# Nine inputs of a chain of attentions turned by VectorE and transfers instead of TensorE

## The chip, the cores and the metric

The kernel runs on one core of a Trainium2 chip. The metric is the time of one execution on the device, in microseconds. All arithmetic is in float32; the scores of two of the three layers use products in which a float32 is split in a high and a low part.

## The reference

Sixteen batches of 256 tokens with 256 features pass three attentions and a feed-forward layer. Softmax, norms and heads are the usual ones; the mask is all ones.

```python
def _L0_xattn_ref(query, context, context_mask, Wq, Wk, Wv, Wo, g_q, g_c, g_out):
    ...
    Q = (q_norm @ Wq)   # 16 heads of 16 features
    K = (c_norm @ Wk)
    V = (c_norm @ Wv)
    ...
    attn = jax.nn.softmax(scores, axis=-1)
    ...
    return rmsnorm(query + out, g_out)

def _forward(x, y, ...):
    h = _ln(x, ln1_g, ln1_b)
    q, k, v = ...                      # of h; q and k are rotated (rope)
    a = _attn(q, k, v, causal=True)
    x = x + (a @ sa_wo + sa_bo)
    h = _ln(x, ln2_g, ln2_b)
    q = ...                            # of h; k and v of y
    a = _attn(q, k, v, causal=False)
    x = x + (a @ ca_wo + ca_bo)
    h = _ln(x, ln3_g, ln3_b)
    return x + (jax.nn.gelu(h @ fc1_w + fc1_b) @ fc2_w + fc2_b)
```

Layer 0 is the cross attention with rms norms, layer 1 the causal self attention, layer 2 the cross attention to y. The last stage is the feed-forward layer, 256 to 1024 to 256.

## The kernel before

There are 48 attentions, 0 to 47: 3 layers by 16 batches. ORDER says which layer each number belongs to, so that the batches run as staggered pipelines: attention 5 is layer 1 of batch 0, 38 is layer 1 of batch 13, 47 is layer 2 of batch 15, the last. The feed-forward layer follows for pairs of batches (class Mlp, 8 pairs); its products are arranged as seven products instead of eight per level (up 1 to 7, down 1 to 7), with sums formed by VectorE (mix, sum_a).

Nothing is left to a scheduler. Each attention is cut in named words: stats, norm, q, k, v, four steps of scores (three for the causal layer), values, take_last, sums_in, heads_in, invert, divide, project, finish. A word is a generator with a step for each engine's part. The string PLAN lists 2640 such steps by name; the kernel walks through it and each word named does its next step. So PLAN is the order of every engine's queue at once: TensorE runs the first steps of q, k, v, scores, values and project in the order in which they stand there, and an instruction whose input is late holds up all that is behind it on its engine. SP's DMA queue is in order in the same way. Behind PLAN stands the code of the last stage, a loop over the pairs.

A layer's input x lies with tokens in the partitions. The products by q, k and v need it with features in the partitions, so after norm (L555) the tile xn must be turned. There are two ways:

- turn: four TensorE transposes with the identity into one PSUM bank (turn_ps, L570), and one copy to the tile hT (turn_out, L577), by ScalarE for attentions and by VectorE for the pairs 0 and 1.
- pieces: VectorE transposes blocks of 32 by 32 (pieces, L586, two instructions for an input), one transfer writes the tile bits to the DRAM tensor turn_hop (pieces_out, L594), and four transfers read it back so that the blocks come to the right partitions (pieces_in, L600). All five transfers are on SP's queue.

Before the change 15 inputs are turned (attentions 5, 12, 18, 22, 31, 38, 43, 45, 47, and both inputs of the pairs 0, 1 and 2) and 33 go in pieces (23 attentions and five pairs). The third pair is turned in the loop of the last stage, later pairs go in pieces there.

The scores (L955, L966) fill a PSUM tile for each half of the heads in a step; the pool psS has two such tiles, so one step fills it. ScalarE empties each with an exponential (L978), then values (L1009) multiplies the result with V. Other transfers on SP's queue bring the parts of q and k to the pairs of rows that the split products read (q_out L842, k_out L889), the heads and sums of an attention to the layout of the projection (heads_in L1032, sums_in L1043), and the inverses of the sums through DRAM (invert L1056, L1062; inv_hop, inv). divide (L1069) multiplies, project (L647) is the product with the output weights.

Of the kernel before, what the change touches and what calls it, by code (L numbers as in the profile page):

```python
# [55 lines left out]
scores.0.1 stats_x.2 values.0.0 q.1 scores.0.2 stats_y.2 v.1 scores.0.2 stats_y.2 scores.0.2  # L56
stats_x.3 values.0.1 load_piece.5.0 scores.0.3 stats_x.2 k.1 scores.0.3 stats_x.3 send.2 stats_y.3
scores.0.3 k.2 v.1 load_piece.5.1 v.1 send.2 k.1 values.0.1 send.3
scores.1.0 k_high.2 k_low.2 load_early.4 q.2 scores.1.0 send.3 scores.1.0 values.0.2 receive.2
load_early.3 scores.1.1 k_out.2 values.0.3 scores.1.1 q.3 q.2 scores.1.1 take_last.0 load_early.0  # L60
q_high.2 scores.1.2 q_low.2 values.1.0 scores.1.2 q_low.2 heads_in.0 v.2 v.2 stats_y.6 scores.1.2
q_out.2 scores.1.3 v.2 sums_in.0 k.3 stats_x.6 scores.1.3 receive.3 scores.1.3 load.4 values.1.1
k_high.3 values.1.1
scores.2.0 invert.0 values.1.2 k_low.3 scores.2.0 q.3 values.1.3 scores.2.0 heads_in.0 take_last.1
q_high.3 scores.2.1 invert.0 v.3 v.3 k_out.3 q_low.3 stats_x.6 scores.2.1 q_low.3 sums_in.1
scores.2.1 stats_y.3 values.2.0 stats_x.4 scores.2.2 stats_x.4 q_out.3 k.4 scores.2.2
load_piece.6.0 send.4 v.3 send.4 scores.2.2 load_piece.5.3 values.2.1 send.6 divide.0 k_high.4
stats_y.4 scores.2.3 invert.0 q.4 invert.1 scores.2.3 k_low.4 scores.2.3 receive.4 invert.1
stats_x.8 values.2.1
scores.3.0 heads_in.1 stats_x.8 values.2.2 scores.3.0 heads_in.1 fold_of_att load_piece.6.1  # L70
scores.3.0 q.4 load_early.2 load_later.1 values.2.3 divide.0 stats_y.4 q_high.4 invert.1
scores.3.1 send.8 take_last.2 project.0 scores.3.1 q_low.4 k_out.4 q_low.4 scores.3.1 values.3.0
project.0 fold_of_att q_out.4 scores.3.2 project.0 v.4 v.4 divide.1 scores.3.2 stats_y.8 project.0
scores.3.2 values.3.1 load_piece.5.2 finish.0 fold_of_att load_piece.7.2 scores.3.3 stats.5
values.3.1 k.6 scores.3.3 v.4 stats.5 scores.3.3 values.3.2 load_piece.7.0 sums_in.2 norm.5
k_high.6
scores.4.0 load_piece.7.1 k_low.6 values.3.3 scores.4.0 divide.1 fold_of_att turn.5 take_last.3
scores.4.0 send.6 project.1 fold_of_att turn.5 sums_in.3 invert.2 scores.4.1 heads_in.2 divide.2
project.1 load_later.0 q.5 project.1 scores.4.1 heads_in.2 fold_of_att project.1 scores.4.1
values.4.0 invert.2 invert.3 q.5 load_piece.6.2 scores.4.2 finish.1 heads_in.3 k.5 scores.4.2 q.5  # L80
q.5 load_early.1 scores.4.2 invert.3 values.4.1 q.5 receive.6 k.5 q.5 scores.4.3 k_out.6
values.4.1 q.6 k.5 q.5 q.5 invert.2 k.5 scores.4.3 v.5 v.5 stats_y.6 k.5 scores.4.3 k.5 heads_in.3
load_piece.6.3 values.4.2 q.6 stats.7
scores.5.0 q_high.6 values.4.3 stats.7 q_low.6 scores.5.0 v.6 q_low.6 scores.5.0 take_last.4
scores.5.0 q_out.6 divide.2 scores.5.0 send.8 scores.5.1 v.5 divide.3 v.6 norm.7 project.2
# [265 lines left out]
def xattn_kernel(  # L351
# [744 lines left out]
    def run(steps):  # L1096
        for _ in steps or ():
            pass
# [57 lines left out]
    class Mlp:  # L1156
# [31 lines left out]
        def pieces_out(self):  # L1188
            self.hops = [pieces_out(pieces(xn)) for xn in self.xns]
# [328 lines left out]
    with tc.manual_schedule():  # L1518
# [38 lines left out]
        for g in range(B // 2):  # L1557
# [56 lines left out]
            if third is not None:  # L1614
                third.pieces_out()
# [451 lines left out]
```

## Time and profile before

| | |
|---|---|
| median of 3 runs | 880.16 us (880.13 to 881.4) |
| the profiled execution | 880.08 us, its span 878.4 us |
| TensorE busy | 867.9 us, 99% of the span |
| VectorE busy | 660.0 us, 75% |
| ScalarE busy | 593.4 us, 68% |
| GpSimd busy | 352.9 us, 40% |
| granted TensorE clock | 1.00 |
| attention stage (PLAN) | to about 672 us |
| last stage | about 672 us to the end |

A row of the profile names the line, the engine, the operation and the tiles; x is the number of instructions, then come busy time, mean duration in ns, and the idle time of the engine just before them with what ended it. A float32 product shows as two records, a transpose by TensorE as one. In a timeline, the first number is the start in the span and the second the duration. SPq is the DMA queue of SyncE: its durations are those of issuing, not of the transfer.

### The profile page before, as it was taken

How to read it: one execution, taken by the hardware profiler on the slowest of the kernel's cores; microseconds unless marked ns; L12 is line 12 of the kernel's file. 1: busy time of each engine (PE TensorE's matmuls, PEld its weight loads, DVE VectorE, ACT ScalarE, POOL GpSimd, SP SyncE). 2: the span in 40 equal slices, each digit the busy share in tenths (PEclk: the TensorE clock that was granted, in tenths of full speed). 3: DMA queues.
4: the chain of work that ended last, by engine and by line, in shares of the span. 5: the costliest groups of instructions: out<-in, count | busy, mean ns of one | idle time of the engine just before them, and what ended most of it. 6: DMA issues, size and time to landing. Idle time of an engine off the chain costs nothing.

```text
span 878.4 us, 32887 instructions
## 1 busy us (share of the span) xinstructions
PE 867.9 (99%) x13762; PEld 558.9 (64%) x13762; DVE 660.0 (75%) x1487; ACT 593.4 (68%) x848; POOL 352.9 (40%) x558
## 2 busy tenths in 40 slices
PE   8999999999999999999999999999999999999997
PEld 4455555555555555555555555555556899999997
DVE  5368888888787878788776788888784787787562
ACT  4788767877787877788777787788876733333440
POOL 4154685257355357264555534334152132222000
PEclk9999999999999999999999999999999999999999
DMA  8576465455344345443343333224331022211201
GB/s 275 182 225 189 134 182 178 148 164 167 117 153 131 110 138 169 144 132 118 126 134 125 113 115 131 95 83 155 124 110 52 14 72 73 67 55 30 69 25 51
DMA packets 101454, 107.04 MB, mean 122 GB/s; under 512 B 26602, under 2 KB 81778, under 8 KB 101298
## 3 DMA queue, kind: packets, MB, share of 16 engines
q1 hardware_dynamic: 96210, 89.89, 31.1%
q0 software_dynamic: 4400, 14.42, 5.6%
q8 instruction: 110, 1.80, 0.9%
q10 hardware_dynamic: 688, 0.54, 0.2%
q14 instruction: 46, 0.38, 0.1%
HBM read 46.33 MB, written 13.65 MB: 68 GB/s over the span
## 4 chain that ended last, share of the span: by engine, by line
PE 86%; DVE 4%; DMA 3%; issue 2%; SPq 2%; ACT 2%; POOL 1%; ACTq 0%; DVEq 0%; POOLq 0%
PE d L647 17%; PE d L635 16%; PE A L1009 15%; PE S L966 8%; PE upX L1223 6%; PE S L955 6%; PE A L1321 6%; PE downZ L1321 3%; PE upZ L1223 3%; PE d L1321 2%; PE d L1223 2%; ACT pt L978 1%; PE d L570 1%; PE downX L1321 1%; DMA hT<-turn_hop 1%
## 5 line engine op out<-in xcount | busy, mean ns | idle before, releaser
L978 ACT ACTIVATE pt<-S 128x1024 f32<-128x1024 f32 x224 | 218.6, 1025 | 87.7 <-PE S L955 56.5
L1009 PE MATMUL A<-pt,va 128*32 128x256 f32 (+1 forms) x3072 | 183.1, 362 | 0.1
L978 ACT ACTIVATE pt<-S,sy 128x1024 f32<-128x1024 f32 x128 | 137.0, 1116 | 28.6 <-PE S L966 16.1
L1009 PEld LDWEIGHTS A<-pt,va 128*32 128x32 f32 x3072 | 94.3, 110 | 63.9 <-issue 7.4
L986 POOL TENSOR_SCALAR_AFFINE_SELECT pt<-pt 128x512 f32<-128x512 f32 x128 | 94.4, 757 | 77.3 <-ACT pt L978 76.7
L966 PEld LDWEIGHTS S<-qm,kT 32*128 32x128 f32 x1920 | 66.6, 183 | 49.6 <-issue 23.6
L966 PE MATMUL S<-qm,kT 32*128 32x256 f32 x1920 | 92.6, 303 | 1.5 <-ACT pt L978 1.3
L623 POOL TENSOR_TENSOR cur<-cur,bias 128x512 f32<-128x512 f32 x48 | 63.8, 1334 | 39.4 <-DVE xn L555 39.2
L527 POOL TENSOR_SCALAR r_ln<-bmv 128x2 f32<-128x2 f32 x48 | 15.6, 325 | 138.5 <-DVE bmv L546 137.4
L1024 ACT COPY av<-A 128x512 f32<-128x512 f32 x96 | 56.6, 590 | 20.6 <-PE A L1009 20.4
L1245 ACT COPY g<-upX 128x512 f32<-128x512 f32 x28 | 15.0, 589 | 72.4 <-issue 68.1
L955 PE MATMUL S<-qm,kT 32*64 32x512 f32 (+1 forms) x1152 | 63.5, 512 | 0.0
L635 PE MATMUL d<-hT,sa 128*32 128x256 f32 x1024 | 61.4, 381 | 0.4 <-DMA hT<-turn_hop 0.4
L762 ACT ACTIVATE a<-d,qk_bias 128x256 f32<-128x256 f32 x128 | 53.9, 477 | 4.6 <-PE d L635 4.4
L555 DVE TENSOR_SCALAR xn<-cur,bmv,r_ln 128x256 f32<-128x256 f32 x96 | 49.2, 561 | 5.3 <-POOL r_ln L528 5.3
L776 DVE TENSOR_TENSOR a<-a,turn 128x512 f32<-128x512 f32 x64 | 48.5, 758 | 1.6
L1261 ACT ACTIVATE g<-g,fb 128x256 f32<-128x256 f32 x96 | 41.0, 499 | 11.1 <-DVE g L1250 11.1
L776 DVE TENSOR_TENSOR u<-u,turn 128x512 f32<-128x512 f32 x64 | 47.8, 747 | 0.0
L770 DVE STREAM_SHUFFLE u<-a 128x512 f32<-128x512 f32 x64 | 47.4, 740 | 0.3 <-issue 0.2
L635 PEld LDWEIGHTS d<-hT,sa 128*32 128x32 f32 x1024 | 30.8, 109 | 24.0 <-issue 3.4
L1069 DVE TENSOR_TENSOR oT<-oT,inv 128x512 f32<-128x512 f32 x48 | 35.9, 749 | 11.3 <-issue 5.5
L1067 POOL TENSOR_TENSOR seen<-seen,sums 128x64 f32<-128x64 f32 x48 | 19.4, 404 | 57.2 <-DVE sums L1053 50.6
(175 smaller groups left out, 1667.7 us busy)
## 6 DMA issues: line engine op xcount, KB each, us to landing
kT<-hl SPq DMA_DIRECT2D x60, 256.0 KB
qm<-qm SPq DMA_DIRECT2D x60, 256.0 KB
oT<-av SPq DMA_DIRECT2D x192, 64.0 KB
inv<-inv_hop SPq DMA_DIRECT2D x96, 128.0 KB
turn_hop<-bits SPq DMA_DIRECT2D x33, 256.0 KB
hT<-turn_hop SPq DMA_DIRECT2D x92, 64.0 KB
out<-res SPq DMA_DIRECT2D x15, 256.0 KB
cur<-in_x POOLq DMA_DIRECT2D x11, 256.0 KB, 3.5
```

The source lines that it names most:

```text
L623: nc.gpsimd.tensor_tensor(t, t, bias_sb[:, row : row + D].unsqueeze(1).to_broadcast([P, NC, D]), ALU.add)
L635: nc.tensor.matmul(o, lhsT=w[:, k, at + t * P + j : at + t * P + j + 32], rhs=tokens, start=(k == 0), stop=(k == KC - 1), skip_group_check ...
L647: nc.tensor.matmul(ps[j : j + 32, c * D : (c + 1) * D], lhsT=some_tokens(src, k, c, j), rhs=w[:, k, at : at + D], start=(k == 0), stop=(k ...
L776: nc.vector.tensor_tensor(t, t, table.unsqueeze(1).to_broadcast([P, KC, S]), ALU.mult)
L955: nc.tensor.matmul(ps[64 * half : 64 * half + 64, 2 * m * u : 2 * m * (u + 1)] .rearrange("p (i s) -> p i s", i=2), lhsT=self.kT[r, t, at] ...
L966: nc.tensor.matmul(ps[:, at : at + m], lhsT=self.kd[r, i, t, kc * P : (kc + 1) * P].bitcast(F32R), rhs=self.qd[r, i, h, t, q0:S].bitcast(F ...
L978: nc.scalar.activation(pt[:, :, :w], ps[:, :, :w], AF.Exp, scale=scale)
L986: nc.gpsimd.affine_select(out=diag, in_=diag, compare_op=ALU.is_ge, fill=0.0, base=0, pattern=[[0, 2], [0, 2], [1, P]], channel_multiplier=-1,
L1009: nc.tensor.matmul(self.av[32 * r : 32 * r + 32, i, q0:S], lhsT=self.va[:, kc, 8 * t + 2 * r + i, :], rhs=pts[r // 2][:, r % 2, i * m : (i ...
L1024: copy(av, self.av)
L1223: nc.tensor.matmul(o if len(b.shape) == 2 else by_groups(o), lhsT=a[:, c * P : (c + 1) * P], rhs=b, start=(first and c % 2 == 0), stop=Tru ...
L1321: nc.tensor.matmul(ps[:, c, :], lhsT=a[f // 2][:, f % 2, c * P : (c + 1) * P], rhs=b[:, f, :], start=(first and c == 0 and f == 0), stop=True,
```

## The change

Five attentions (5, 22, 31, 38, 47) and the pairs 0 and 1 of the last stage, nine inputs in all, go in pieces instead of being turned. In PLAN their words turn become pieces and pieces_in; the words of the pairs are mlp.n.pieces_out and mlp.n.pieces_in. Mlp.pieces_out becomes a generator with a step for each part, and the loop of the last stage runs it to its end. PLAN, now 2647 steps, is written anew: with the same words apart from these, in another order from the first line to the last. Attentions 12, 18, 43, 45 and the pair 2 are turned as before. All line numbers behind PLAN move up by three.

The diff, with PLAN cut to two stretches: attentions 2 to 4, in which attention 5 is prepared, and 44 to 47.

```diff
 PLAN = """
...
-scores.2.0 invert.0 values.1.2 k_low.3 scores.2.0 q.3 values.1.3 scores.2.0 heads_in.0 take_last.1
-q_high.3 scores.2.1 invert.0 v.3 v.3 k_out.3 q_low.3 stats_x.6 scores.2.1 q_low.3 sums_in.1
-scores.2.1 stats_y.3 values.2.0 stats_x.4 scores.2.2 stats_x.4 q_out.3 k.4 scores.2.2
-load_piece.6.0 send.4 v.3 send.4 scores.2.2 load_piece.5.3 values.2.1 send.6 divide.0 k_high.4
-stats_y.4 scores.2.3 invert.0 q.4 invert.1 scores.2.3 k_low.4 scores.2.3 receive.4 invert.1
-stats_x.8 values.2.1
-scores.3.0 heads_in.1 stats_x.8 values.2.2 scores.3.0 heads_in.1 fold_of_att load_piece.6.1
-scores.3.0 q.4 load_early.2 load_later.1 values.2.3 divide.0 stats_y.4 q_high.4 invert.1
-scores.3.1 send.8 take_last.2 project.0 scores.3.1 q_low.4 k_out.4 q_low.4 scores.3.1 values.3.0
-project.0 fold_of_att q_out.4 scores.3.2 project.0 v.4 v.4 divide.1 scores.3.2 stats_y.8 project.0
-scores.3.2 values.3.1 load_piece.5.2 finish.0 fold_of_att load_piece.7.2 scores.3.3 stats.5
-values.3.1 k.6 scores.3.3 v.4 stats.5 scores.3.3 values.3.2 load_piece.7.0 sums_in.2 norm.5
-k_high.6
-scores.4.0 load_piece.7.1 k_low.6 values.3.3 scores.4.0 divide.1 fold_of_att turn.5 take_last.3
-scores.4.0 send.6 project.1 fold_of_att turn.5 sums_in.3 invert.2 scores.4.1 heads_in.2 divide.2
-project.1 load_later.0 q.5 project.1 scores.4.1 heads_in.2 fold_of_att project.1 scores.4.1
-values.4.0 invert.2 invert.3 q.5 load_piece.6.2 scores.4.2 finish.1 heads_in.3 k.5 scores.4.2 q.5
-q.5 load_early.1 scores.4.2 invert.3 values.4.1 q.5 receive.6 k.5 q.5 scores.4.3 k_out.6
-values.4.1 q.6 k.5 q.5 q.5 invert.2 k.5 scores.4.3 v.5 v.5 stats_y.6 k.5 scores.4.3 k.5 heads_in.3
-load_piece.6.3 values.4.2 q.6 stats.7
+scores.2.0 v.2 k_high.3 values.1.2 heads_in.0 k_low.3 scores.2.0 values.1.3 scores.2.0 invert.0
+v.3 k_out.3 v.3 divide.0 take_last.1 stats_x.6 q_high.3 sums_in.1 scores.2.1 stats_x.4
+load_piece.6.0 k.4 scores.2.1 stats_x.4 invert.0 scores.2.1 load_piece.7.0 values.2.0 send.4
+q_low.3 send.4 fold_of_att scores.2.2 q_low.3 stats_y.6 values.2.1 scores.2.2 q_out.3 invert.1
+scores.2.2 stats_x.8 heads_in.1 values.2.1 v.3 stats_x.8 scores.2.3 invert.1 k_high.4 q.4
+receive.4 divide.0 scores.2.3 load_piece.6.1 fold_of_att send.6 send.8 load_later.1 k_low.4
+scores.2.3 values.2.2 load_piece.5.3 stats_y.4
+scores.3.0 q.4 project.0 k_out.4 scores.3.0 scores.3.0 values.2.3 heads_in.1 project.0 q_high.4
+scores.3.1 project.0 fold_of_att v.4 scores.3.1 q_low.4 project.0 invert.1 q_low.4 scores.3.1
+divide.1 finish.0 q_out.4 load_piece.5.2 take_last.2 scores.3.2 stats.5 values.3.0 scores.3.2
+stats_y.8 stats.5 values.3.1 scores.3.2 stats_y.4 norm.5 values.3.1 scores.3.3 pieces.5 stats_y.6
+k.6 divide.1 pieces.5 scores.3.3 sums_in.2 fold_of_att v.4 scores.3.3 values.3.2 fold_of_att
+heads_in.2 k_high.6
+scores.4.0 v.4 values.3.3 pieces_in.5 scores.4.0 k_low.6 project.1 invert.2 scores.4.0 send.6
+take_last.3 scores.4.1 project.1 sums_in.3 values.4.0 project.1 scores.4.1 invert.2 q.5 project.1
+scores.4.1 heads_in.2 load_piece.7.1 finish.1 scores.4.2 q.5 send.8 divide.2 k.5 invert.3
+load_piece.6.3 scores.4.2 q.5 invert.2 scores.4.2 q.5 values.4.1 q.5 k.5 scores.4.3 receive.6 q.5
+invert.3 q.6 load_early.2 q.5 q.5 load_early.1 k.5 k_out.6 scores.4.3 k.5 v.5 values.4.1 k.5
+scores.4.3 heads_in.3 k.5 values.4.2 q.6 heads_in.3
...
-scores.44.0 invert.42 q.45 values.43.3 k_high.45 scores.44.0 heads_in.42 q.45 v.45 v.45 q.45
-scores.44.0 q.45 scores.44.1 take_last.43 q_high.45 k_low.45 k.46 sums_in.43 scores.44.1 v.45
-q_low.45 scores.44.1 values.44.0 k_out.45 divide.42 k.46 scores.44.2 q_low.45 project.41
-scores.44.2 q_out.45 invert.43 k.46 scores.44.2 invert.43 k.46 values.44.1 k.46 scores.44.3
-values.44.1 project.41 q.46 heads_in.43 scores.44.3 k.46 scores.44.3 heads_in.43 values.44.2
-k_high.46
-scores.45.0 invert.43 q.46 k_low.46 values.44.3 scores.45.0 q.46 project.42 take_last.44
-scores.45.0 q.46 sums_in.44 q.46 scores.45.1 q.46 v.46 v.46 divide.43 k_out.46 scores.45.1
-divide.43 keep.44 project.42 scores.45.1 heads_in.44 values.45.0 stats.47 keep.46 q_high.46
-values.45.1 invert.44 stats.47 scores.45.2 q_low.46 invert.44 k.47 q_low.46 scores.45.2 norm.47
-q_out.46 scores.45.2 v.46 keep.47 turn.47 heads_in.44 mlp.0.stats k.47 scores.45.3 keep.43 turn.47
-invert.44 q.47 scores.45.3 k.47 mlp.0.stats scores.45.3 k.47 values.45.1 k.47
+scores.44.0 k.45 invert.42 values.43.3 k.45 scores.44.0 q.45 v.45 v.45 scores.44.0 divide.42 q.45
+take_last.43 q.45 scores.44.1 k_high.45 sums_in.43 k_low.45 k.46 scores.44.1 v.45 k_out.45
+scores.44.1 q.45 divide.42 k.46 scores.44.2 k.46 project.41 scores.44.2 invert.43 k.46 invert.43
+scores.44.2 values.44.0 k.46 q_high.45 heads_in.43 project.41 scores.44.3 k.46 q.46 q_low.45
+k_high.46 q_low.45 values.44.1 k_low.46 q_out.45 q.46 project.42 scores.44.3 heads_in.43 q.46
+scores.44.3 q.46 k_out.46 k.47 q.46 values.44.1 q.46 heads_in.44 project.42 values.44.2 q_high.46
+stats.47
+scores.45.0 k.47 invert.43 values.44.3 q_low.46 scores.45.0 stats.47 v.46 q_low.46 scores.45.0
+divide.43 norm.47 v.46 combine.5 take_last.44 pieces.47 scores.45.1 k.47 pieces.47 keep.46
+scores.45.1 q_out.46 mlp.0.stats scores.45.1 sums_in.44 keep.45 scores.45.2 k.47 values.45.0
+mlp.0.stats scores.45.2 pieces_in.47 divide.43 values.45.1 scores.45.2 k.47 k.47 values.45.1
+keep.44 scores.45.3 invert.44 values.45.2 mlp.0.norm invert.44 scores.45.3 divide.44 q.47
+scores.45.3 heads_in.44 mlp.0.pieces_out k_high.47
-scores.46.0 q.47 k.47 values.45.2 divide.44 scores.46.0 q.47 values.45.3 scores.46.0 divide.44
-q.47 k_high.47 scores.46.1 take_last.45 project.44 q.47 scores.46.1 sums_in.45 q.47 scores.46.1
-k_low.47 values.46.0 q_high.47 k_out.47 scores.46.2 v.47 v.47 q_low.47 scores.46.2 q_low.47
-scores.46.2 mlp.0.norm q_out.47 values.46.1 scores.46.3 project.44 mlp.0.keep project.43 invert.45
-scores.46.3 invert.45 values.46.1 scores.46.3 mlp.0.turn project.43 heads_in.45 keep.45
-values.46.2 v.47 heads_in.45 mlp.0.turn
-scores.47.0 mlp.0.turn mlp.1.stats invert.45 scores.47.0 values.46.3 scores.47.0 take_last.46
-scores.47.1 mlp.1.stats sums_in.46 mlp.0.up2 scores.47.1 heads_in.46 scores.47.1 divide.45
-divide.45 values.47.0 mlp.0.turn scores.47.2 mlp.1.norm project.45 scores.47.2 invert.46
-scores.47.2 invert.46 values.47.1 heads_in.46 project.45 scores.47.3 mlp.0.mix values.47.1
-mlp.1.turn scores.47.3 invert.46 values.47.2 scores.47.3 mlp.1.turn mlp.1.turn values.47.3
-mlp.1.turn
+scores.46.0 mlp.0.pieces_out k_low.47 q.47 invert.44 values.45.3 scores.46.0 q.47 k_out.47
+scores.46.0 q.47 v.46 take_last.45 scores.46.1 q.47 sums_in.45 project.43 mlp.0.pieces_out
+scores.46.1 q.47 scores.46.1 mlp.0.pieces_out divide.44 q_high.47 scores.46.2 project.44 q_low.47
+scores.46.2 q_low.47 scores.46.2 mlp.1.stats q_out.47 values.46.0 heads_in.45 scores.46.3 v.47
+v.47 invert.45 scores.46.3 mlp.1.stats heads_in.45 project.44 scores.46.3 project.43 invert.45
+values.46.1 divide.45
+scores.47.0 mlp.1.norm mlp.0.pieces_in values.46.1 combine.7 values.46.2 scores.47.0 v.47 keep.47
+values.46.3 scores.47.0 take_last.46 mlp.0.keep scores.47.1 invert.45 values.47.0 scores.47.1
+sums_in.46 scores.47.1 mlp.0.mix scores.47.2 mlp.0.up2 scores.47.2 invert.46 divide.45 invert.46
+scores.47.2 heads_in.46 mlp.1.pieces_out values.47.1 scores.47.3 mlp.1.pieces_out mlp.1.pieces_out
+values.47.1 project.45 invert.46 scores.47.3 mlp.1.pieces_out scores.47.3 values.47.2 project.45
+values.47.3 mlp.1.pieces_in heads_in.46
...
 """
...
         def pieces_out(self):
-            self.hops = [pieces_out(pieces(xn)) for xn in self.xns]
+            self.hops = []
+            for n, xn in enumerate(self.xns):
+                if n:
+                    yield
+                t = pieces(xn)
+                yield
+                self.hops.append(pieces_out(t))
...
             if third is not None:
-                third.pieces_out()
+                run(third.pieces_out())
```

## The prediction

> **What bounds the kernel now.** I read the page first (busy times, slices, shares of the chain), then the groups kept apart by shape, then the timelines of TensorE, ScalarE and the DMA queue around the turns, last the chain of waits.
>
> ```profile
> span 878.4 us, 32887 instructions
> ...
> PE 867.9 (99%) x13762; PEld 558.9 (64%) x13762; DVE 660.0 (75%) x1487; ACT 593.4 (68%) x848; POOL 352.9 (40%) x558
> ...
> PE   8999999999999999999999999999999999999997
> ...
> PEclk9999999999999999999999999999999999999999
> ...
> PE 86%; DVE 4%; DMA 3%; issue 2%; SPq 2%; ACT 2%; POOL 1%; ACTq 0%; DVEq 0%; POOLq 0%
> ```
>
> TensorE is busy in every slice at full clock and holds 86% of the chain: a microsecond of TensorE work taken out is a microsecond of time, unless TensorE then waits. The span allows 10.5 us of idle TensorE in all. The next two lines are the two ways to turn an input: four TensorE transposes (L570), or two VectorE ones (L586) and a trip through DRAM.
>
> ```profile
> L570 PE MATMUL d<-ident,xn 128*128 128x128 f32 x60 | 9.9, 286 | 0.5 <-DVE xn L555 0.4
> ...
> L586 DVE STREAM_TRANSPOSE bits<-xn 128x256 f32<-128x256 f32 x66 | 24.5, 413 | 0.2
> ```
>
> The TensorE timeline of the last stretch shows what a turn takes of the queue, and what a step of scores needs:
>
> ```profile
> 655.54 0.66 PE L570 MATMUL d<-ident,xn 128*128 128x128 f32 x4
> 656.13 1.07 PE L1009 MATMUL A<-pt,va 128*32 128x256 f32 x16
> 657.13 0.75 PE L966 MATMUL S<-qm,kT 32*128 32x256 f32 x16
> 657.80 0.66 PE L570 MATMUL d<-ident,xn 128*128 128x128 f32 x4
> 658.39 1.07 PE L1009 MATMUL A<-pt,va 128*32 128x256 f32 x16
> 659.39 0.39 PE L966 MATMUL S<-qm,kT 32*128 32x256 f32 x2
> 659.96 0.74 PE L966 MATMUL S<-qm,kT 32*128 32x256 f32 x14 [0.18 <-ACT pt L978]
> 660.63 1.99 PE L1223 MATMUL d<-mT,fc 128*128 128x256 f32 x8
> ```
>
> A turn takes 0.59 us from start to start. Pitches of the other words, read in the same way: q, k, v, project 1.75; scores 0.68; values 0.97. The second thing to see: scores.47.0 starts at 657.13, scores.47.1 is held by ScalarE and is through at 660.63, as if it had started at 659.93. Both PSUM tiles of a step must be emptied first, by ScalarE:
>
> ```profile
> 657.97 1.94 ACT L978 ACTIVATE pt<-S 128x1024 f32<-128x1024 f32 x2 [1.70 <-PE S L966]
> ```
>
> So two steps of scores are at least 2.8 us apart, even with ScalarE free. TensorE must have 2.1 us of other work between them or it waits: here it had values.46.3 and a turn, 1.56, and lost about 0.5.
>
> Last, what the way through DRAM takes: a write and its read on the DMA queue, and the worst read of the chain.
>
> ```profile
> 192.99 0.32 SPq L594 DMA_DIRECT2D turn_hop<-bits  x1
> ...
> 195.34 1.88 SPq L600 DMA_DIRECT2D hT<-turn_hop  x4
> ```
>
> ```profile
> 115.16 5.59 DMA hT<-turn_hop
> 120.75 0.14 issue
> 120.88 1.97 PE d L635 x32
> ```
>
> **What is removed.** Nine turns by 0.59 = 5.3 us of TensorE, all of it on the path. I add 0.4 for waits of TensorE at the turns themselves that go with them (the excess over the pitch at turn.38 and turn.47). ScalarE loses five copies of 0.59 (2.95), VectorE four copies of 0.69 (2.75). [...]Credit 5.7.
>
> A rule of the Trainium skill speaks against the exchange ("VectorE: DVE Perf Modes", "Rules for kernel authors"): turn full 128x128 blocks on TensorE, since VectorE only turns 32x32 blocks inside a bank. Its section "The three transpose paths" puts one such TensorE transpose (bf16) at 390 ns. An input would then be worth 4 x 0.39 = 1.56 us and nine 14.0, where the row gives 0.59 and 5.3; I take the row. What the rule warns of is the missing reordering of blocks, here the trip through DRAM.
>
> **What is added.** Per input: two VectorE transposes (0.83 by their mean, 0.77 as a pair), one write and four reads on SP's queue. VectorE: 9 x 0.83 = 7.4 minus 2.75, about 5 us more in 878. Before these places it is 75% busy and TensorE waits for it 1.5 us in the whole run, so 0; in the last 40 us, where it is 90% busy, the 0.77 stands in the chains below. SP's queue: 9 x (0.34 + 1.85) = 20 us more issue time; it is in order, so heads, sums, inverses, q_out and k_out behind each read are 1.8 us later. Their consumers stand 14 us or more behind in TensorE's order (values to project) or 7.9 (k to scores, the same minimum as before), so 0, but for one place: mlp.1.pieces_in issues eight reads (3.7 us) ahead of the second heads_in.46, for which project.46 waits. From scores.47.3 TensorE has project.45, two values, up 1, 5, 6 = 9.2 us; the queue needs 3.7 + 1.2 + a landing of 2.5 + divide 0.7 = 8.1. It fits by 1.1: 0, up to 2 with a landing like the chain's worst. DMA volume grows by 9 x 512 KB, 4%: 0. The generator form of Mlp.pieces_out, run to its end in the loop, leaves the order there as it was: 0.
>
> **What the trip costs in latency.** Transposes 0.77; write 2.35 (192.99 to the read that waits for it, 195.34); three reads ahead of the last 1.4; landing of the last 2.8 (the chain has 2.83 for inv<-inv_hop, another read back from DRAM) to 5.6 (the row above). That is 7.3 to 10.1 us after norm, against 1.45 from turn.47 (639.63) to q.47 (641.08). The skill's "DMA: Bandwidth & Descriptors", "Anatomy of one DMA", gives 2.0 us fixed plus bytes over 436 GB/s, written for another queue: 2.6 and 2.15, so 0.8 + 2.6 + 1.4 + 2.15 = 6.9. The page would let att 47 below off by 0.4; I use the rows.
>
> Where is that hidden? Add TensorE's pitches between the last project that the input needs and its first consumer. Of the 23 attentions already in pieces the shortest is 25.4 us. After the change: att 47, project.42 to q.47, 12.8; att 5, project.0 to q.5, 16.2; att 38, project.32 to k.38, 19.5. The others have 24 or more: 0.
>
> Att 47: at best 1.85 (project) + 0.7 (add) + 1.1 (statistics) + 1.9 (POOL root) + 1.15 (norm) + 7.3 = 14.0, so 1.2 short; with the queueing that before shows (project.42 to q.47 took 10.3, 8.9 without its turn) 8.9 + 7.3 = 16.2, 3.4 short. I take 2.4.
> Att 5: project.0 to the end of norm took 9.1 (58.53 to 67.6); with 7.3, 16.4; with the late landing 19.2: short by 0.2 to 3.0, I take 1.3, since SP's queue and the DMA engines are fullest there.
> Att 38: 9.1 + 7.3 = 16.4 of 19.5: 0, at worst 0.6.
>
> **What the new order costs.** PLAN is new throughout. I walked both lists for neighbouring scores with under 2.8 us from start to start. Before, three places (scores.2.3 to 3.0, 45.3 to 46.0, 47.0 to 47.1) lack 1.3 together. After, seven: 2.2 to 2.3 has only values.2.1 between (lacks 1.15), 3.1 to 3.2 (0.4), 44.1 to 44.2 (0.4), 45.1 to 45.2 with nothing between (2.1), 46.0 to 46.1 (1.15), 46.1 to 46.2 (0.4), 47.1 to 47.2 (1.15): 6.75. 3.1 to 3.2 lies inside att 5's wait and 45.1 to 45.2 inside att 47's; they cover one another, so 6.75 - 0.4 - 2.1 = 4.25 stays beside those waits. Less the 1.3: 2.95 more. Bounds: 1 (if other waits fall into the same gaps) to 4.
>
> **The sum.** -5.7 + 1.3 + 2.4 + 2.95 = +0.95. Against the profiled execution's own 880.08 (span 878.4) that is 881.0; the median of the runs, 880.16, lies 0.1 above the profiled one, so it stands for both: 881.0. Best of every term: -5.7 + 0.2 + 1.2 + 1 = -3.3, 876.8. Worst, with 2 at project.46 and 0.6 at att 38: -5.7 + 3.0 + 3.4 + 4 + 2.6 = +7.3, 887.4.
>
> **The cases.** A measurement of this kernel can tell about 0.2%, 1.8 us, from no change: 878.4 to 881.9 is "same".
> A, exchanged one for one (0.42): TensorE's 5.7 us come back as waits for ScalarE and for the trip; 881.0, its own range 878.4 to 881.9. For it: TensorE's slack is in the same stretches where the work is taken out. Against: gaps may merge.
> B, the gain is kept (0.18): q.47 and q.5 come at their best and the gaps merge, or much of before's own idle 10.5 goes; 877.3. For it: the first four turns (5, 22, 31, 38) lie where TensorE is at 99 to 100%, and 2.4 of 5.3 is due there whatever the end does.
> C, slower (0.40): the last read lands late. Place: hT of att 5 and att 47. Price: each us beyond 2.8 is a us of TensorE, since q stands in order before scores, values and project. With 4.5 instead of 2.8 at both: 881.0 + 3.4 = 884.4. It decides from a landing of 3.3 on (+0.9 in sum). For it: the chain has 5.59 for this very read, while DMA is half busy; SP's queue is longer now. Against: at 570 to 578 us att 42 lived on 9.5 us from its transposes to q without a wait.
> D, the change doesn't do what it says: TensorE would have waited at the turns anyway. Partly true for the pairs (their 2.4 us filled gaps of scores 46 and 47), and counted in A through the gaps; it gives 880 to 881.
>
> Range for 8 in 10: 877.5 to 885.5. It leaves out the ends of B and C.
>
> **What would show it.** In the profile after: the turns (L570, three lines up after the change) at x24 instead of x60; VectorE's transposes at x84 instead of x66; TensorE's busy time about 5 less and its idle 5 to 6 more; waits of q (L635) for hT<-turn_hop or for xn's chain near 72 and 641 us, 1 to 3 each; ScalarE holding the scores at 2.3, 45.2, 46.1, 47.2; scores.44.0 2 us earlier than before's 615.6, but the first up product of the last stage at 672 to 674. Wrong if TensorE's idle stays near 10.5 (then 875 to 876), or if waits stand elsewhere: at project for inverses, or at scores for q_out and k_out behind the reads.

## The result, and the profile after

The changed kernel took 890.7 us (median of 4 runs, 887.3 to 893.3) against 880.67 for the kernel before beside it: 1.0110 times as long, 95% interval 1.0089 to 1.0131. It is slower by 1.1%, outside the range that the prediction gave. The profiled execution took 890.79, of which the span is 889.1; against the span of before, 878.4, that is 10.7 us more. Lines of the code have moved up by three (turn: L567; pieces: L583; write and read: L591 and L597), those of the last stage down by three.

The page after, the rows that answer to those of before (busy time, TensorE by slices, its clock, the chain):

```profile
span 889.1 us, 32882 instructions
...
PE 865.6 (97%) x13726; PEld 557.7 (63%) x13726; DVE 672.7 (76%) x1501; ACT 591.1 (66%) x843; POOL 351.7 (40%) x558
...
PE   8999989999999999999999999999988999999997
...
PEclk9999999999999999999999999999999999999999
...
PE 34%; DVE 1%; SPq 1%; ACT 1%; DMA 1%; issue 0%; POOL 0%; ACTq 0%; POOLq 0%
```

TensorE has 36 transposes less, and its idle time (span less busy) has grown from 10.5 to 23.5 us. The chain covers 38% of the span here, since it could be followed back no further; it says nothing of the first half, and the waits have to be found in another way. The groups by shape show that the exchange itself is what the diff says, 36 transposes gone and 18 halves added:

```profile
L583 DVE STREAM_TRANSPOSE bits<-xn 128x256 f32<-128x256 f32 x84 | 31.2, 413 | 0.3
...
L567 PE MATMUL d<-ident,xn 128*128 128x128 f32 x24 | 3.7, 282 | 0.0
```

Where TensorE waits is the table of waits (us in total, times, longest):

```profile
PE S L963 <- ACT pt L975: 5.8, 10, 1.1
PE d L644 <- DVE oT L1066: 5.2, 3, 2.6
...
PE A L1006 <- DVE va L927: 1.2, 1, 1.2
...
PE d L632 <- DVE sums L1050: 0.7, 1, 0.7
PE d L632 <- DMA hT<-turn_hop: 0.6, 1, 0.6
```

The trip through DRAM, on which the prediction spent most of its care, is in the last two rows: 0.6 at q.5, and 0.7 at q.47, which the trace puts down to sums although q reads hT and not sums. The large rows are scores held by ScalarE (1.3 before) and three projections (project.4, 9 and 46) that wait for their divided values (0.3 before). At project.4 the division waits for the inverse, at project.46 for the heads (oT<-av in the trace); at project.9 the trace names a transfer that the division does not read, so what held it is open.

To place them I took, for every TensorE word of PLAN, its start to the start of the next, less the median pitch of its kind in the profile of before, and added these excesses up by stretches of the span. Negative entries are pitches below the median. All columns come from one profiled execution each; e1 to e12 are the experiments below, by the start of their labels.

| us from start | before | after | e1 | e2 | e4 | e5 | e10 | e12 |
|---|---|---|---|---|---|---|---|---|
| 0-86 | 1.8 | 4.0 | 4.1 | 3.4 | 3.7 | 3.3 | 3.4 | 3.1 |
| 86-105 | -0.3 | 0.1 | -0.4 | 4.7 | 0.6 | 4.7 | 0.2 | -0.4 |
| 105-125 | 0.2 | 4.2 | 0.5 | 0.0 | 2.6 | 0.0 | 1.2 | 0.7 |
| 125-200 | 0.6 | 1.2 | 0.6 | 0.8 | 0.4 | -0.3 | 0.4 | 1.0 |
| 200-400 | -0.8 | -1.7 | -1.6 | -1.5 | -1.9 | -1.7 | -1.4 | -1.6 |
| 400-430 | -0.5 | 1.4 | 1.4 | 0.1 | 3.0 | 0.1 | 0.2 | 0.3 |
| 430-530 | -0.5 | -0.7 | -1.0 | -0.6 | -0.6 | -0.6 | -0.7 | -0.7 |
| 530-560 | -0.1 | 2.0 | 1.2 | 0.0 | 2.1 | 0.0 | -0.1 | -0.1 |
| 560-620 | -0.6 | -0.7 | -0.8 | -0.8 | -0.7 | -0.7 | -0.6 | -0.6 |
| 620 to the end of PLAN | 3.5 | 8.0 | 6.7 | 7.9 | 8.3 | 7.5 | 8.0 | 6.7 |
| sum | 3.3 | 17.9 | 10.6 | 14.0 | 17.6 | 12.2 | 10.6 | 8.3 |

The account closes: 17.9 - 3.3 = 14.6 us of new waiting, less nine turns of 0.59 (5.3), is 9.3, and the last word of PLAN starts at 680.7 instead of 671.4. From there to the end it is 208.4 us instead of 207.0: 1.4 more, and 9.3 + 1.4 = 10.7.

Three places of the profile after carry what the prediction did not have. First, project.4 at 113 to 120 us, from the timelines of VectorE (the division), of SP's queue and of TensorE, and the clock by stretches (last three columns: granted clock, DMA share, GB/s):

```profile
115.96 0.69 DVE L1066 TENSOR_TENSOR oT<-oT,inv 128x512 f32<-128x512 f32 x1 [4.05 <-DMA inv<-inv_hop]
```

```profile
104.94 2.05 SPq L1053 DMA_DIRECT2D inv_hop<-sums  x2
109.28 1.29 SPq L1059 DMA_DIRECT2D inv<-inv_hop  x2
```

```profile
116.71 3.49 PE L644 MATMUL d<-w0o,oT 128*32 128x256 f32 x32 [2.61 <-DVE oT L1066]
```

```profile
112.00:116.00 4.00, 2.10 (x36) 0.62 (x28) 0.04 (x1) 1.83 (x2) 1.22 (x2) 1.00 0.72 230
116.00:120.00 4.00, 3.29 (x32) 1.58 (x36) 2.62 (x7) 1.16 (x2) 1.16 (x3) 0.57 0.95 200
```

The reciprocal of attention 4 is done at 104.4; its inverse comes back 11.6 us later, 5.4 us after the read was issued, in a stretch where the DMA engines are 72% busy. TensorE waits 2.61, and then the projection itself takes 3.49 us instead of 1.93, because the clock is granted at about half (0.57 over the stretch from 116 to 120): 4.2 us at one place.

Second, 414 us. VectorE's addition that makes hl takes 0.69 alone. Here it takes 3.25, and lasts as long as a chain of GpSimd operations beside it (timelines of VectorE, GpSimd, ScalarE):

```profile
414.24 3.25 DVE L862 TENSOR_TENSOR hl<-a,u 128x512 f32<-128x512 f32 x1
```

```profile
414.39 0.65 POOL L983 TENSOR_SCALAR_AFFINE_SELECT pt<-pt 128x512 f32<-128x512 f32 x1
414.98 0.17 POOL L925 MEMSET va<- 128x32 f32 x1
415.05 0.64 POOL L983 TENSOR_SCALAR_AFFINE_SELECT pt<-pt 128x512 f32<-128x512 f32 x1
415.66 1.27 POOL L620 TENSOR_TENSOR cur<-cur,bias 128x512 f32<-128x512 f32 x1
```

```profile
417.52 0.62 ACT L874 CAST hl<-hl 128x512 fp32r<-128x512 f32 x1 [2.17 <-DVE hl L862]
```

ScalarE waits 2.17 for it, with the exponentials queued behind, and the next scores are late by 1.84 in two steps. L620 is the word keep, moved here by the new list. The Trainium skill has the mechanism ("SBUF — State Buffer", "Who interferes with whom"): a VectorE instruction with two inputs in SBUF contends with a GpSimd instruction that reads SBUF, for ports that only one of them can hold. What the trace adds is that several GpSimd instructions in a row were waited out together here, though by the records the addition began 0.15 us before the first of them.

Third, 542 us. The tile for the pieces, bits, shares its two buffers (tag "a") with ScalarE's biased q and k, and is free only when its write to DRAM has been done:

```profile
539.44 1.37 SPq L591 DMA_DIRECT2D turn_hop<-bits  x1
```

```profile
542.62 0.84 ACT L759 ACTIVATE a<-d,qk_bias 128x256 f32<-128x256 f32 x2 [2.65 <-DMA turn_hop<-bits]
```

The new list has 17 words between the two halves of pieces.40, where the old had five. The pieces were made by 536.1, the write went out at 539.44 behind an inverse's write, and ScalarE stood for 2.65. Pieces.40 is not one of the nine: it went through DRAM before as well.

### The profile page after: what moved, and what is told of

Same layout as the page of the kernel before. It is cut to its first block, busy times and chain, and to the rows that moved or that the text cites. A ratio compares the mean times of both kernels' runs of the same rounds, so it can differ in the third digit from the quotient of the medians.

```text
span 889.1 us, 32882 instructions
## 1 busy us (share of the span) xinstructions
PE 865.6 (97%) x13726; PEld 557.7 (63%) x13726; DVE 672.7 (76%) x1501; ACT 591.1 (66%) x843; POOL 351.7 (40%) x558
## 5 line engine op out<-in xcount | busy, mean ns | idle before, releaser
L975 ACT ACTIVATE pt<-S,sy 128x1024 f32<-128x1024 f32 x128 | 136.8, 1116 | 31.3 <-PE S L963 17.6
L983 POOL TENSOR_SCALAR_AFFINE_SELECT pt<-pt 128x512 f32<-128x512 f32 x128 | 88.1, 707 | 96.5 <-ACT pt L975 96.0
L963 PEld LDWEIGHTS S<-qm,kT 32*128 32x128 f32 x1920 | 67.4, 183 | 54.4 <-ACT pt L975 23.5
L620 POOL TENSOR_TENSOR cur<-cur,bias 128x512 f32<-128x512 f32 x48 | 64.7, 1353 | 30.7 <-DVE xn L552 30.6
L552 DVE TENSOR_SCALAR xn<-cur,bmv,r_ln 128x256 f32<-128x256 f32 x96 | 55.0, 620 | 5.8 <-POOL r_ln L525 5.8
L1066 DVE TENSOR_TENSOR oT<-oT,inv 128x512 f32<-128x512 f32 x48 | 32.7, 681 | 16.9 <-DMA inv<-inv_hop 5.9
L1319 DVE TENSOR_TENSOR g<-g,g 128x512 f32<-128x512 f32 x64 | 40.5, 680 | 0.0
```

What stands on the lines that cost most here:

```text
L552: nc.vector.tensor_scalar(xn[:, c, :], src[:, c, :], mv[:, c, 0:1], r[:, c : c + 1], ALU.subtract, ALU.mult,)
L620: nc.gpsimd.tensor_tensor(t, t, bias_sb[:, row : row + D].unsqueeze(1).to_broadcast([P, NC, D]), ALU.add)
L963: nc.tensor.matmul(ps[:, at : at + m], lhsT=self.kd[r, i, t, kc * P : (kc + 1) * P].bitcast(F32R), rhs=self.qd[r, i, h, t, q0:S].bitcast(F ...
L975: nc.scalar.activation(pt[:, :, :w], ps[:, :, :w], AF.Exp, scale=scale)
L983: nc.gpsimd.affine_select(out=diag, in_=diag, compare_op=ALU.is_ge, fill=0.0, base=0, pattern=[[0, 2], [0, 2], [1, P]], channel_multiplier=-1,
```

## The experiments

Theory 1: the new order of PLAN costs the time, in places that have little to do with the nine inputs. Theory 2: the added transfers cost it, through SP's longer queue.

**e1_order_only: the order without the exchange.** The changed list, with the nine inputs turned on TensorE:

```diff
-values.3.3 pieces_in.5 scores.4.0 k_low.6 project.1 invert.2
+values.3.3 turn.5 scores.4.0 k_low.6 project.1 invert.2 turn.5
```

> The changed kernel's list of words, with the nine inputs turned on TensorE again, each in one place of that list (where its read stood, or the write in the last pair): no added VectorE turn, no added transfer. Theory 1, the new order itself costs: the mid-plan waits of the changed kernel (4.2 us at 113-120, 1.2 at 183, 1.8 at 417, 2.5 at 536-550) stay, the nine turns come back with 5.3, the waits for the trips (0.7 at q.5, 1 to 2 at q.47) go: 890.7 + 5.3 - 2.2 = 893.8, between 892 and 896. Theory 2, the added transfers cost (SP's queue longer by 20 us, late hops): these waits go with them, and only the starved scores stay: 880.2 + 3 = 883, between 881 and 885.

Measured 888.17 (887.0 to 891.3), 1.0099 times before (1.0075 to 1.0122). It lies between the two expectations. The order alone costs 8.0 us; exchanging the nine in this order costs 2.5 more by the medians, though it takes 5.3 us of TensorE out. The 8.0 is clear of the scatter. The 2.5 is not: four runs each, 887.0 to 891.3 here and 887.3 to 893.3 in the changed kernel. Its table of waits has the scores first (the same columns as above), and nearly nothing for inverses:

```profile
PE S L963 <- ACT pt L975: 6.9, 13, 1.1
...
PE d L644 <- DVE oT L1066: 1.3, 2, 0.9
```

In the column e1 the waits at 0-86, at 400-430, part of 530-560 and most of the tail are there without one added transfer; those at 105-125 are not.

**e4_tail_turned: the tail undone.** Attention 47 and the pairs turned, 5, 22, 31 and 38 through DRAM.

```diff
-scores.45.2 pieces_in.47 divide.43 values.45.1 scores.45.2 k.47
+scores.45.2 turn.47 divide.43 values.45.1 scores.45.2 k.47 turn.47
```

> The changed kernel's list with only the tail undone: attention 47 and the two pairs of the last stage are turned on TensorE again, attentions 5, 22, 31 and 38 keep their trips. Theory 1, order: five turns come back with 2.95, the wait for hT at q.47 and the reads at the end go (1.5 to 2): 890.7 + 1.2 = 892, between 890 and 894. Theory 2, transfers, above all those in the full last 40 us: the tail's 7.0 us of waits fall to the 3.0 of the kernel before, less is gained by the turns: 890.7 - 4.0 + 2.95 = 889.6 at most, 887 to 890.

Measured 890.93 (890.6 to 891.6), as theory 1 had it. So the five turns of the tail bring nothing that these runs can tell, and the 2.8 us between this and e1 (with e1's scatter, a rough figure) are those of four inputs, of which two have 24 us or more in hand and a third 19.5. They go to the same kind of place: project.4 waits 2.52 here too, and the stretch 400-430 has 3.0. In this execution project.4 then ran at full clock; the half clock came at 417.94, after two waits for ScalarE in a row, as the timeline of TensorE shows:

```profile
416.35 0.38 PE L963 MATMUL S<-qm,kT 32*128 32x256 f32 x2 [0.89 <-ACT pt L975]
417.27 0.74 PE L963 MATMUL S<-qm,kT 32*128 32x256 f32 x14 [0.53 <-ACT pt L975]
417.94 3.25 PE L644 MATMUL d<-ca,yT 128*32 128x256 f32 x32
```

The changed kernel had the same two waits (0.87 and 0.53 at 419 to 420) and kept its full clock there.

**e2_words_moved: seven words of the changed list moved, all transfers kept.**

```diff
-load_piece.9.0 ... load_later.3 ... load_later.4 ... load_later.5 project.4
+project.4 ... project.5 load_later.5 load_later.4 load_later.3 load_piece.9.0
-pieces.40 (17 words) pieces.40
+pieces.40 scores.37.2 divide.35 values.37.1 pieces.40
-keep.31 scores.29.0 ... keep.30 scores.29.1
+scores.29.2 keep.31 ... scores.30.0 keep.30
```

> The changed kernel with all its transfers, seven words moved: four weight and input loads from before project.4 to behind project.5, the second half of pieces.40 (the write of bits) from 16 words behind the first to 4, keep.31 and keep.30 to where they stand in the kernel before. Theory 1, order: the waits at 113-120 (4.2), at 540 (2.5) and at 417 (1.8) go, 8.5 us at best: 882.2; with half of it given back in new waits 886; between 882 and 887. Theory 2, transfers: the waits come of SP's longer queue and turn up in the next place: 889 to 891.

Measured 886.89 (883.2 to 887.7), the upper end of theory 1. The three places are mended in the table: 0.0 at 105-125, 0.1 at 400-430, 0.0 at 530-560. The second shows what GpSimd does to VectorE: with the addition of keep.31 (1.27) moved away and the two selects still beside it, hl takes 2.00 instead of 3.25.

```profile
414.13 2.00 DVE L862 TENSOR_TENSOR hl<-a,u 128x512 f32<-128x512 f32 x1
```

But 4.7 us stand at 86-105, where no word was moved, so half of the gain had not arrived.

**e5_mended: three more things in the tail.** Besides e2's words: k.47 moved between scores.45.1 and 45.2, which had no TensorE work between them; keep.47 and mlp.0.keep moved behind values.47.2; the eight reads of pair 1 moved behind the last heads_in.46.

```diff
-values.47.3 mlp.1.pieces_in heads_in.46
+values.47.3 heads_in.46 mlp.1.pieces_in
```

> The changed kernel with the seven words of e2_words_moved moved, and three more things in its tail: k.47 on TensorE moved from before scores.45.0 to between scores.45.1 and scores.45.2, which stood with nothing between them; keep.47 and mlp.0.keep (three additions of 512 on GpSimd, back to back, beside which VectorE's norm of pair 1 took 5.34 us instead of 2.1) moved from before scores.47.1 to behind values.47.2; mlp.1.pieces_in (eight reads) moved behind the last heads_in.46. Theory 1, the order places it wrongly: from e2's 886.9 go 1.2 at scores.45.2, 1.2 at values.47.0 (the wait for va behind that norm) and 1.4 in the last stage (208.8 us there against 206.9 without the pairs' reads): 883.1, between 881.5 and 884.5. Theory 2, what is mended comes back in the next place: 885.5 to 887.5.

Measured 882.28 (20 runs, 878.4 to 885.9), 1.0021 times before (1.0011 to 1.0032). Theory 1. The last stage falls from 208.4 to 207.0, as before the change: the reads ahead of heads_in.46 had cost the 1.4 us, at this wait of the changed kernel's timeline of TensorE, where project.46 starts:

```profile
688.46 1.93 PE L644 MATMUL d<-cao,oT 128*32 128x256 f32 x32 [1.40 <-DVE oT L1066]
```

Moving keep.47 and mlp.0.keep did nothing. GpSimd has no work queued ahead of them at the new place either and ran them at the same point, 5 us before TensorE got there; VectorE's norm of pair 1 took 5.34 us beside them, as in the changed kernel (1.37 in the kernel before). Where nothing ahead of a word on its own engine waits, as here, another place in the list does not move it in time.

**e6_order_mended: the same mending, with the nine turned on TensorE.** The diff is e1's and e5's together, without the words that e1 lacks; the four loads stay where they are.

> e1_order_only (the changed list, all nine inputs turned on TensorE) with the same mending, as far as it applies: keep.31, keep.30, the second half of pieces.40, k.47, keep.47 and mlp.0.keep. Theory 1, order: the places at 416 (1.2), 540-545 (1.0) and 640 (1.2) go: 888.2 - 3.4 = 884.8, between 883.5 and 886. If each trip costs more than its turn wherever it stands, e5_mended is 2 to 3 us slower than this one, as the changed kernel is against e1_order_only (890.7 against 888.2); if it was the places that the trips happened to meet, e5_mended is as fast or faster by 1 to 2.

Measured 883.48 (883.0 to 884.2), 1.0040 times before (1.0025 to 1.0055). By the medians the exchange cost 2.5 us in the list as it came and gains 1.2 in the mended list. What is shown is that the trips as such do not cost the 10.5: with all nine kept, moving a dozen words took the time from 890.70 to 882.28. That the exchange turned from a loss to a gain is likely, not shown: the 2.5 is within the scatter, the 1.2 just outside it (four runs of e6), and e5 differs from e6 also in the four loads and in the place of the last heads_in.46. Of 5.3 us, 1.2 is the most that is seen to arrive.

**e10_one_word: the place at 86-105.** In e2 and e5 VectorE's second square of y took 3.37 us beside GpSimd's selects, and va of attention 5 stood behind it (timelines of VectorE, GpSimd and TensorE of e5_mended):

```profile
90.79 3.37 DVE L532 SCALAR_TENSOR_TENSOR sq<-y 128x256 f32<-128x256 f32 x1
```

```profile
90.43 0.81 POOL L983 TENSOR_SCALAR_AFFINE_SELECT pt<-pt 128x512 f32<-128x512 f32 x1
91.22 0.31 POOL L1064 TENSOR_TENSOR seen<-seen,sums 128x64 f32<-128x64 f32 x1
91.49 2.40 POOL L983 TENSOR_SCALAR_AFFINE_SELECT pt<-pt 128x512 f32<-128x512 f32 x4
```

```profile
94.92 1.51 PE L1006 MATMUL A<-pt,va 128*32 128x256 f32 x12 [3.29 <-DVE va L927]
```

In the changed kernel the same instructions stood at the same place, and the square took 0.73 (timelines of VectorE and GpSimd of the changed kernel).

```profile
91.22 0.73 DVE L532 SCALAR_TENSOR_TENSOR sq<-y 128x256 f32<-128x256 f32 x1
```

```profile
90.85 0.81 POOL L983 TENSOR_SCALAR_AFFINE_SELECT pt<-pt 128x512 f32<-128x512 f32 x1
91.64 0.48 POOL L1064 TENSOR_TENSOR seen<-seen,sums 128x64 f32<-128x64 f32 x1
```

The distance does not explain it: the square started 0.37 us after the select there and 0.36 after it in e4, where it took 0.73 too, and 0.36 after it in e2 and e5, where it took 3.38 and 3.37. What decides, and with it over 3 us of TensorE, the traces do not show. The edit puts va first:

```diff
-take_last.4 norm.7 v.5 load_piece.6.2 scores.5.1 sums_in.4 stats_y.10 scores.5.0 project.2 v.5
+take_last.4 norm.7 v.5 load_piece.6.2 scores.5.1 sums_in.4 scores.5.0 project.2 v.5 stats_y.10
```

> e5_mended with one word moved, the first stats_y.10 to behind the last v.5. VectorE still meets the four GpSimd selects, but the addition for va stands ahead of the squares. If a VectorE operation that starts beside a chain of GpSimd operations is held to the chain's end, and the wait of 3.3 us at values.5.0 came of that: that wait and the half clock after it go, 882.3 - 3 to 5: 878.5, between 877 and 879.5. If the wait came of something else (the transfers, the matrix v.5): 881.5 to 883.

Measured 881.60 (22 runs, 879.7 to 883.6), 1.0011 times before (1.0004 to 1.0019). The wait is gone, as the timelines of VectorE and GpSimd show:

```profile
89.96 0.71 DVE L927 TENSOR_TENSOR va<-d,bias 128x512 f32<-128x512 f32 x1
...
91.03 0.42 DVE L532 SCALAR_TENSOR_TENSOR sq<-y 128x256 f32<-128x256 f32 x1
```

```profile
91.15 2.76 POOL L983 TENSOR_SCALAR_AFFINE_SELECT pt<-pt 128x512 f32<-128x512 f32 x4
```

Two later squares stood beside the same four selects and took 0.65 and 0.73, so a row of GpSimd instructions does not always hold VectorE to its end. Yet the median fell by 0.7 only, which is within the scatter, and the expectation of 3 to 5 was wrong. Two things fit. The runs of e5 reached from 878.4 to 885.9, those of e10 from 879.7 to 883.6: the profiled execution of e5, 883.89, was one of its longer ones, and the edit took the longest away. And TensorE now reaches project.4 some 4 us earlier than in e5 and waits 1.1 for the inverse there (1.2 in the table), where e2 and e5 had none. So e2's zero at 105-125 was bought in part with its 4.7 at 86-105, and how much of project.4's 2.61 the moved loads took is open: 1.5 by this profile.

**e9_mended_more: three further words** (v.47 ahead of mlp.1.norm, combine.5 ahead of norm.47, values.2.0 behind scores.2.2) on top of e10's.

> e5_mended with four more words moved: the first stats_y.10 (VectorE's squares of y, for which nobody waits at once) from before v.5's addition to behind it; v.47's addition from behind mlp.1.norm to before it; combine.5 (1.35 us of GpSimd beside the norm of attention 47) from before that norm to behind project.42, where GpSimd is idle; values.2.0 from before scores.2.2 to behind it. Theory 1, the places decide: in e5's profiled execution (883.89) 5.0 us were lost at 90-100 (VectorE's square of y took 3.37 us instead of 0.42 beside four GpSimd selects, va of attention 5 behind it, values.5.0 waited 3.3, and a stretch at half clock followed), 1.2 at values.47.0 and up to 0.9 at q.47: with these gone 877, between 875.5 and 879, which is faster than the kernel before (880.4). Theory 2, mended places come back elsewhere: 880.5 to 882.5.

Measured 881.83 (879.6 to 884.1): no gain over e10. The wait for va at values.47.0 went (it is in no row of its profile), but q.47 still waited 1.55 and the scores behind values.47.0 took the rest up. The mended place came back next door, as theory 2 had it.

**e11_five_turned and e12_ends_turned: e10, with 5, then 5 and 47 turned on TensorE again.**

```diff
-values.3.3 pieces_in.5 scores.4.0
+values.3.3 turn.5 scores.4.0
-scores.45.2 pieces_in.47 divide.43
+scores.45.2 turn.47 divide.43
```

> e10_one_word with attention 5 turned on TensorE again, everything else as there (trips for 22, 31, 38, 47 and the two pairs). Project.4 waited 2.6 us in both profiles that had a trip for 5 in the unmended list (changed kernel, e4_tail_turned), 1.1 in e10, and 0 to 0.5 in those with 5 turned (e1, e6). If the trip of 5 is what makes the inverse of attention 4 late, the 1.1 at project.4 and the 0.4 at q.5 go and 0.59 comes back: 881.6 - 0.9 = 880.7, between 880 and 881.3. If it is chance of the landing, project.4 still waits 1 and the time is 881.8 to 882.5.

> As e11_five_turned, and attention 47 is turned on TensorE too: trips remain only where there is slack (22, 31, 38) and for the two pairs. The wait of 1.66 for hT at q.47 goes for a turn of 0.59: 1.1 less than e11, 879.6, between 878.8 and 880.4; that would be the first version below the kernel before (880.4). If the wait at q.47 only moves to the scores behind it, which ScalarE holds there anyway: 880.5 to 882.

Measured 881.31 (1.0015 times before, 1.0006 to 1.0023) and 880.70 (1.0004, 0.9994 to 1.0013). E11 stands at the edge of its main expectation (880 to 881.3), e12 missed it: it is level with before and not below. In e11 project.4 does not wait, in e12 it waits 1.0 with attention 5 turned just the same. So the wait there can come by the chance of a landing, and my reading that the trip of 5 alone makes it was wrong. That the trip adds to it is neither shown nor excluded: of the four executions with 5 turned (e1, e6, e11, e12) one waits there, 1.0; of the six with the trip in the new list four wait (changed kernel 2.6, e4 2.5, e9 1.3, e10 1.1), and the other two (e2, e5) had lost over 3 us at 90 to 95.

**In the order of before.** Three kernels put trips into the old list and leave all else.

e3_two_in_place, attentions 22 and 31, which have slack:

```diff
-norm.22 v.20 v.20 scores.19.0 scores.19.1 ... finish.14 turn.22 ... turn.22
+norm.22 v.20 v.20 pieces.22 scores.19.0 pieces.22 scores.19.1 ... finish.14 pieces_in.22
```

> The kernel before with its own order, and only attentions 22 and 31 turned by VectorE and a trip: the two pieces a word or two behind norm, the read where the first half of the turn stood, nothing else moved. Theory 1, order: the trip is hidden (about 18 and 44 us from norm to the first consumer), so two turns of 0.59 are gained: 880.2 - 1.2 = 879.0, between 878.3 and 879.8. Theory 2, transfers: SP's queue is 4.4 us longer and something behind it waits: 880.2 to 882.

Measured 880.23 (14 runs) against 880.17: ratio 0.9999, 0.9991 to 1.0007. The transfers are hidden, and the gain of 1.2 does not show. In its profiled execution 0.4 of the 1.2 came back as excess within 200 to 430 us, where the two turns had stood; a rest of up to 0.8 is below what the runs can tell.

e7_five_in_place, all five attentions:

```diff
-norm.5 k_high.6 scores.4.0 ... fold_of_att turn.5 ... turn.5
+norm.5 pieces.5 pieces.5 k_high.6 scores.4.0 ... fold_of_att pieces_in.5
```

> The kernel before with its own order, and all five attentions (5, 22, 31, 38, 47) turned by VectorE and a trip in place: the pieces right behind norm, the read where the first half of the turn stood; the pairs stay turned. The waits that the new order was written to avoid: with 7.3 to 10.1 us from norm to hT, q.5 (72.3 without its turn, norm done at 67.6) waits 2.6 to 5.4, k.38 (511.8, norm done at 506.1) 1.6 to 4.4, q.47 (640.5, norm done at 639.6) 6.4 to 9.2; 10.6 to 19 in all, less five turns of 0.59: 888 to 896, most likely 890. If waits in the same stretch (3.7 us of held scores in the tail) merge with these: 885 to 888.

Measured 895.51 (894.0 to 898.7), 1.0168 times before (1.0150 to 1.0187). This is what the new list was written to avoid. Two places, q.5 and q.47, hold most of it. The timeline of TensorE at q.5, and the clock there:

```profile
78.75 3.64 PE L635 MATMUL d<-hT,sa 128*32 128x256 f32 x32 [5.78 <-DMA hT<-turn_hop]
```

```profile
76.00:80.00 4.00, 1.25 (x13) 0.68 (x16) 0.00 (x0) 0.00 (x0) 1.90 (x4) 0.73 0.63 179
80.00:84.00 4.00, 4.00 (x40) 1.79 (x32) 1.91 (x6) 0.84 (x2) 0.00 (x0) 0.50 0.33 100
```

q.5 waited 5.78 (2.6 to 5.4 expected), q.47 6.02 (6.4 to 9.2), k.38 0.5 (1.6 to 4.4). The first two are each followed by a stretch at half clock that costs another 2.8 and 1.6.

e8_pairs_in_place, the two pairs alone:

```diff
-scores.46.2 mlp.0.norm q_out.47 values.46.1
+scores.46.2 mlp.0.norm mlp.0.pieces_out mlp.0.pieces_out q_out.47 values.46.1
```

> The kernel before with its own order, and only the two pairs of the last stage turned by VectorE and trips: pair 0's pieces behind its norm and its read at the second word of its turn, pair 1's pieces at the words of its turn and its read at the end of the list. Theory A, a turn is worth its 0.59 wherever it stands: four of them are 2.4, the reads ahead of project.46 cost 1.4 in the last stage: 880.2 - 1.0 = 879.2. Theory B, a turn between two steps of scores is cover for ScalarE's exponentials: nothing is gained where the scores are held anyway, the last stage costs 1.4 more: 881.6, between 880.7 and 883.

Measured 885.17 (883.9 to 885.6), 1.0056 times before (1.0044 to 1.0068), worse than either theory. The timeline of TensorE shows two waits that I had not put into the expectation:

```profile
657.74 1.06 PE L963 MATMUL S<-qm,kT 32*128 32x256 f32 x16 [1.33 <-DMA qm<-qm]
...
663.04 3.35 PE L1226 MATMUL d<-mT,fc 128*128 128x256 f32 x8 [1.44 <-DMA mT<-turn_hop]
```

Scores.47.0 waits for q_out.47, which stands on SP's queue behind the writes of the pieces; then the first product of pair 0 waits for its reads and runs at half clock (3.35 us instead of 1.99). SP's order does cost, where the consumer is near.

## Why the prediction was wrong, point by point

The sum had two parts: +2.95 for the new order, and -5.7 + 1.3 + 2.4 = -2.0 for the exchange. The runs put about 8.0 and 2.5 in their place (e1, and the changed kernel against e1; the split is as rough as e1's scatter). Both parts failed, and the second failed in sign.

- **The credit, 5.7 (5.3 of it turns):** the count was right (L567 at x24). How much of it arrives is another matter: at most 1.2, between e6 and e5.
- **The trips' latency, 1.3 at att 5, 2.4 at att 47, 0 at att 38:** measured excess 0.7 at q.5, 0.8 at q.47, none at k.38; 2.2 too much. Case C, which named a late hT as the way to be slower, had the right sign by the wrong mechanism. The estimate of 7.3 to 10.1 us from norm to hT was about right: 8.3 for att 5 and 7.4 for att 47 in the changed kernel, 10.7 and 6.5 in e7, each from the end of norm to the start of q.
- **The new order, 2.95:** this step failed by the most, 8.0 where 2.95 stood. Looking for neighbouring scores under 2.8 us apart found the early stretch and the tail, and e1 (order without trips) has 2.3 more than before in 0-86 and 3.2 more from 620 on: 5.5 for the 2.95. But scores are not the only thing that an order starves. E1 has 1.9 more at 400-430 (keep beside hl) and 1.3 more at 530-560 (bits held over 17 words). In time the order is 8.0 of the 10.5.
- **"VectorE: 9 x 0.83 ... so 0":** the added work was not the cost. VectorE was costed as 75% busy, as if its operations had fixed lengths. Beside GpSimd they don't: the longest held operation of before took 1.6 us more than alone; in the changed kernel hl at 414 took 2.6 more, and the four instructions of the norm of pair 1 took 5.34 together, against 1.37 before.
- **"Their consumers stand 14 us or more behind ... so 0" (SP's queue):** a distance in TensorE's order is no margin until the whole path has been subtracted. For project.4 the reciprocal to the inverse took 11.6 us, and 7.6 to 10.5 in e6 and e10. The prediction named this ("at project for inverses") as what would show it wrong, and priced it at 0. How much of it the added transfers make is not settled: in e12 a wait came without the trip of 5, and the longest ones came with it.
- **mlp.1.pieces_in, 0 with a bound of 2:** 1.4, within the bound, and shown by e5.
- **Not in the sum at all:** the half clock after a wait (1.6 at project.4), and the buffers that bits shares with ScalarE.

The error was to cost the new list by one rule and the transfers by their distances, and to let "TensorE waits 1.5 us for VectorE in all of before" stand for the list that replaced it. The trace of before has 1.3 us of such waits; in the changed kernel the like rows come to 6.8 us (oT 5.2, va 1.2, w 0.4). With a dozen words moved and two attentions turned again (e12), the new list with the remaining seven inputs exchanged is level with the kernel before: 880.70 for 880.45. That is what the prediction's case A had for all nine, one microsecond given for another; how much of it is the order and how much the exchange, no run tells apart. No version that I ran beats the kernel before.

## What to carry to other kernels

When an edit comes with a re-written order, run the order without the edit first: here it was 8.0 of 10.5 us, where walking through the list had found 2.95. On a kernel whose bound engine is 99% busy, work taken off it counts only where nothing else ends at the same moment; list what is due next at each place (here at most about a fifth of the sum arrived: 1.2 of 5.3 between e6 and e5, and nothing to be seen of 1.2 in e3). Costs of the other engines are to be read as paths (what GpSimd runs beside it, who holds the buffer, what is ahead in the queue), not as shares.

## What the runs showed of the hardware

- TensorE's clock fell to half after some waits, and the words that followed cost 1.5 to 2.8 us more: after 2.61 us at 116 (changed kernel, clock 0.57 from 116 to 120), 3.29 at 95 (e5, 0.59 from 94 to 98), 5.78 at 79 (e7, 0.50 from 80 to 84). A wait of 2.52 at the same project.4 in e4 did not do it, while waits of 0.89 and 0.53 close together did at 418 (e4) and did not at 420 in the changed kernel. The Trainium skill ("TensorE: Matmul & The Clock Gate", Part 1, "What's actually happening") puts the fall after an idle window of about 3.4 us which runs free. All of these waits but the 5.78 lie below that, and after some of them the clock fell all the same: here the measurement decides.
- A VectorE operation of 0.42 us took 3.37, and one of 0.69 took 3.25, beside four to six GpSimd instructions back to back. With one of these moved away (e2), the second took 2.00. Elsewhere VectorE was let in between: the four instructions of the norm of pair 1 took 1.37 to 1.47 each beside additions of 1.3, and in two kernels the first operation took 0.73 at the same distance from the same select. What decides is open.
- The two reads of the inverse of attention 4 (128 KB each, issued in 1.3 us) were followed by its division 5.4 us after their issue in the changed kernel, 3.9 in e10 and 2.4 in e6, at the same place of nearly the same list. In e6 the division did not wait for them, so they had landed by then.
